# The last image's first residual: its variance by covariance, its sums taken beside other work, and a projection made ahead of the division

## The chip, the cores and the metric

The kernel runs on one core of one Trainium2 chip. The metric is the device time of one execution in microseconds, the median of the runs shown. A core has a matrix engine (PE), a vector engine (DVE), a scalar engine (ACT), a general engine (POOL) and an engine that issues most DMAs (SP). Each executes its instructions in the order of the program, and waits on semaphores of the others.

## The reference

Four images `x` of 256 channels and 64x64 pixels in float32 go through four layers. Each is a residual on a group norm: `x = x + layer(gn(x))`, with 32 groups of 8 channels.

```
gn(v): mean and variance over groups of 8 channels x 4096 pixels
layer 0: xs = relu(group_norm8(conv3x3(v)))
         f = theta(xs)^T phi(xs); y = softmax(f) g(xs)        # 4096 x 4096 per image
         return 0.1 * group_norm8(w_w y) + xs                 # 8 groups of 32 channels
layer 1: linear attention: rmsnorm, q k v, softmax of q over d and of k over n, context, projection, rmsnorm
layer 2: depthwise 3x3 and pointwise 256x256 convolutions with kernels generated from the input
layer 3: a mix of four 256x256 experts, weighted by a softmax from the pooled input
```

The change concerns the end of layer 0 of the last image and the group norm at the head of layer 1: `x1 = x + xs + 0.1 * gn8(w_w y)`, and then mean and variance of `x1` over groups of 8 channels.

## The kernel before

**Tiles.** The 256 channels lie as two halves (`NH` = 2) of 128 partitions, and an image has 4096 columns. A block `q` is 512 queries (eight blocks). A block has 16 steps `m` of 256 keys. In each step PE makes the logits (`logits`, products `pf`, L898), ACT the exponentials `pr` (L899), PE the sum over keys (`py`, L937), and DVE adds the exponentials to `tot` (L124), from which the softmax's sums come.

**The end of a block** is the generator `ended` (L902 to L926), whose pieces are taken in the first steps of the next block. DVE folds `tot` to `inv` (L906); a product with ones, `pss` (L910), gives the sums over partitions; DVE takes the reciprocal (L912) and divides, `yt = py * inv`; PE projects `yt` with the weights `ww_s` to `ps_wy` (L921), ACT copies that to `wt` (L922), DVE takes `bn_stats` of it (L925), and SP writes `wt` to DRAM (`wy_d`).

**The rest of layer 0 and layers 1 to 3** are the generators `nonlocal_out`, `linear_attention`, `generated` and `mixed`, joined in `tail`. `nonlocal_out` norms the projection (`group_finish`, L330 to L356: `bn_aggr`, an averaging product `pm`, `gm` and `ev` on DVE, a second product `pv`, and `rsqrt` on POOL in L217; then `affine`, L365), and adds it to the residual, `big = wy * sc + xs` (in L1009, recorded under the helper's L127), in eight pieces of 128x1024. In the last image `big` is `tpg`, and the residual stays in SBUF in `xp`; the sums of the residual are made by 16 ACT instructions during the last attention (`residual_sums`, L956 to L963), and the variance of the result by eight ACT squares around the mean that is known by then (L1014). `linear_attention` starts with the second `group_finish`; then, for each of eight chunks of 512 columns, ACT norms the tile (`normed`, L1033, squares L1035, DVE adds the halves to `s2`), PE multiplies by the q, k, v weights (L1057) and sums squares over the channels (`norms`, `ps_ss`, L1043, `rinv` on DVE and POOL), ACT makes the exponentials (L1061) and v (L1062), DVE divides q by its sums, and PE turns q and adds to the context (L1076, L1079).

**The order** on every engine is the one in which the program issues its instructions, and is written out by hand. A `Chain` interleaves the tail of image b-1 with the attention of image b, step by step; the last attention runs beside the tail of image 2, and the tail of the last image follows alone (`end`). Sixteen products of image 2's last layer are held back (`held`, `ps_ex` in L1498) and issued in gaps of PE by `fill(n)`; `settle()` issues the additions that belong to them. In the last image's part, 128x1024 tiles are taken in turns from a pool of nine (`k4`) and from four spare pieces of `ra` and `rt`. The last block's `ended` has no further attention to lie beside, and is stepped by the loop:

```
        for part, _ in enumerate(attention):
            if part == 0:
                end.fill(2)
            elif part == 2:
                end.settle()
        run(last)
```

Of the kernel before, what the change touches and what calls it, by code (L numbers as in the profile page):

```python
# [13 lines left out]
P = 128  # L14
# [79 lines left out]
def conv_preact_fast(ctx: ExitStack, tc: tile.TileContext, guard, x, wc, wtpg, ww, wqkv, wout, w1cat, wd2,  # L94
# [235 lines left out]
    def group_finish(st, avg, eps, shift=None):  # L330


        if callable(st):
            mv = st()
        else:
            mv = sp.tile([P, NH, 2], F32, name="mv")
            for h in range(NH):
                nc.vector.bn_aggr(mv[:, h, :], st[:, h, :, :].rearrange("p c s -> p (c s)"))
        if shift is not None:
            tt(mv[:, :, 0], mv[:, :, 0], shift, ALU.add)  # L340
        yield 1
        pm = bank("pm")
        nc.tensor.matmul(pm[:, 0:NH], avg, mv[:, :, 0], start=True, stop=True)
        gm = sp.tile([P, NH], F32, name="gm")
        nc.vector.tensor_copy(gm, pm[:, 0:NH])
        ev = sp.tile([P, NH], F32, name="ev")
        tt(ev, mv[:, :, 0], gm, ALU.subtract)
        tt(ev, ev, ev, ALU.mult)
        tt(ev, ev, mv[:, :, 1], ALU.add)
        yield 1  # L350
        pv = bank("pv")
        nc.tensor.matmul(pv[:, 0:NH], avg, ev, start=True, stop=True)
        rstd = sp.tile([P, NH], F32, name="rstd")
        nc.vector.tensor_scalar(rstd, pv[:, 0:NH], eps, None, ALU.add)  # L354
        rsqrt(rstd, rstd)
        return mv, gm, rstd  # L356
# [530 lines left out]

    def attend(b):

        probs, todo = {}, []  # L890
        st = wy_stats[b] = sp.tile([P, NH, 8, 6], F32, name="wy_st")

        def logits(i):
            q, m = divmod(i, NM)
            pr = k4("pr")
            for s in range(2):
                pf = bank("pf")
                nc.tensor.matmul(pf, phi[:, bass.ts(2 * m + s, P)], theta[:, bass.ts(q, 512)], start=True, stop=True)  # L898
                nc.scalar.activation(pr[:, bass.ts(s, 512)], pf, AF.Exp)  # L899
            probs[i] = pr  # L900

        def ended(q, py, tot):  # L902

            at = b * NQ + q
            inv = wk.tile([P, 512], F32, tag="inv", name="inv")
            nc.vector.scalar_tensor_tensor(inv, tot[:, 0:512], 1.0, tot[:, 512:CH], ALU.mult, ALU.add,  # L906
                                           accum_out=guard[:, 0, at:at + 1])
            yield
            pss = bank("pss")
            nc.tensor.matmul(pss, ones, inv, start=True, stop=True)  # L910
            yield
            nc.vector.reciprocal(inv, pss)  # L912
            yt = k2("yt")
            tt(yt, py, inv, ALU.mult)
            yield
            nc.scalar.activation(junk(), inv, AF.Copy, accum_out=guard[:, 1, at:at + 1])

            wt = k4("wt").rearrange("p (h n) -> p h n", h=NH)
            for h in range(NH):
                ps = bank("ps_wy")  # L920
                nc.tensor.matmul(ps, ww_s[:, bass.ts(h, P)], yt, start=True, stop=True)  # L921
                nc.scalar.copy(wt[:, h, :], ps)  # L922
            yield
            for h in range(NH):
                nc.vector.bn_stats(st[:, h, q, :], wt[:, h, :])  # L925
            nc.sync.dma_start(out=wy_d[b].rearrange("h p n -> p h n")[:, :, bass.ts(q, 512)], in_=wt)  # L926

        logits(0)
        for i in range(NQ * NM):
            q, m = divmod(i, NM)  # L930
            if m == 0:
                py = bank("py")
                tot = k4("tot")
            if i + 1 < NQ * NM:
                logits(i + 1)
            for s in range(2):
                nc.tensor.matmul(py, g[:, bass.ts(2 * m + s, P)], probs[i][:, bass.ts(s, 512)],  # L937
                                 start=(m == 0 and s == 0), stop=(m == NM - 1 and s == 1))
            if m == 1:
                tt(tot, probs[i - 1], probs[i], ALU.add)  # L940
            elif m > 1:
                tt(tot, tot, probs[i], ALU.add)
            for t in todo:
                next(t, None)
            if m == NM - 1:
                todo = [ended(q, py, tot)]
                next(todo[0])
            yield i + 1 < NQ * NM
        for t in todo:
            for _ in t:  # L950
                yield


    res_sum = cp.tile([P, NH], F32, name="res_sum")

    def residual_sums(xs_in):  # L956

        parts = sp.tile([P, NH, N // 512], F32, name="res_parts", bufs=1)
        for h in range(NH):
            for c in range(N // 512):  # L960
                nc.scalar.activation(junk(), xs_in[:, h, bass.ts(c, 512)], AF.Copy, accum_out=parts[:, h, c:c + 1])
                yield
        nc.vector.tensor_reduce(res_sum, parts, AX.X, ALU.add)  # L963


    def nonlocal_out(w, b, big, k4, xs_in):
# [4 lines left out]
        def load_parts(i):  # L971
            c, h = PARTS[i]
            wy = k4("wy")
# [7 lines left out]
        ahead = 2 if xs_in is None else 6  # L981
        parts = [load_parts(i) for i in range(ahead)]
        if xs_in is not None:
            yield 1
        bias = vec_s[:, V_WB, :]
        wmv, gm, rstd = yield from group_finish(wy_stats[b], avg32, 1e-5, bias)
        sc, sh = affine(gm, rstd, vec_s[:, V_G2W, :], vec_s[:, V_G2B, :], bias, 0.1)
        st = stats_tile()
        if xs_in is not None:

            mv = sp.tile([P, NH, 2], F32, name="mv_in", bufs=1)
            centre = sp.tile([P, NH], F32, name="centre", bufs=1)
            squares = sp.tile([P, NH, N // CH], F32, name="squares", bufs=1)
            tt(mv[:, :, 0], wmv[:, :, 0], bias, ALU.subtract)
            tt(mv[:, :, 0], mv[:, :, 0], sc, ALU.mult)
            stt(mv[:, :, 0], res_sum, 1.0 / N, mv[:, :, 0], ALU.mult, ALU.add)
            nc.vector.tensor_scalar(centre, mv[:, :, 0], -1.0, None, ALU.mult)

            def moments():
                nc.vector.tensor_reduce(mv[:, :, 1], squares, AX.X, ALU.add)  # L1000
                nc.vector.tensor_scalar(mv[:, :, 1], mv[:, :, 1], 1.0 / N, None, ALU.mult)
                return mv

            st = moments
        w.fill(2)
        for i, (c, h) in enumerate(PARTS):
            cols = bass.ts(c, CH)
            wy, xs = parts[i]
            stt(big[:, h, cols], wy, sc[:, h:h + 1], xs, ALU.mult, ALU.add)  # L1009
            if i + ahead < len(PARTS):  # L1010
                parts.append(load_parts(i + ahead))
            yield 0.6
            if xs_in is not None:
                nc.scalar.activation(wy, big[:, h, cols], AF.Square, bias=centre[:, h:h + 1], accum_out=squares[:, h, c:c + 1])  # L1014
            else:
                for s in range(2):
                    nc.vector.bn_stats(st[:, h, 2 * c + s, :], big[:, h, bass.ts(2 * c + s, 512)])
            yield 0.6
        w.settle()
        return st, sh  # L1020


    def linear_attention(w, b, big, qT, k4, st, sh, alone):
        _, gm, rstd = yield from group_finish(st, avg8, 1e-5, sh)
# [56 lines left out]

        ahead = normed(0)
        yield 1
        ready = *ahead, None
        last = None
        for c in range(NC):
            if c + 1 < NC:
                ahead = normed(c + 1)
            yield 0.5
# [9 lines left out]
        rk = sp.tile([P, 1], F32, name="rk")  # L1099
# [98 lines left out]
    def generated(w, b, big, k4, st, sh, diag):  # L1198
        mv, gm, rstd = yield from group_finish(st, avg8, 1e-5, sh)

        pivot = sp.tile([P, NH], F32, name="pivot")
# [7 lines left out]
        hs = sp.tile([HT * HP, NC3], F32, name="hs")  # L1209
# [6 lines left out]
        b1n = sp.tile([HT * HP, 1], F32, name="b1n")  # L1216
# [33 lines left out]
        pooled = sp.tile([HT * HP, 1], F32, name="pooled")  # L1250
        nc.vector.tensor_reduce(pooled, hs, AX.X, ALU.add)
        pd = sp.tile([HT * HP, 2 * R], F32, name="pd")
# [5 lines left out]
        pb = sp.tile([P, 2 * R], F32, name="pb")  # L1258
# [3 lines left out]
        dk = sp.tile([P, NH * 9], F32, name="dk")  # L1262
# [177 lines left out]
    def mixed(w, b, big, k4, st, sh, held):  # L1440
# [7 lines left out]
        pool = sp.tile([P, NH], F32, name="rpool")  # L1448
# [6 lines left out]
        hid = sp.tile([EH, 1], F32, name="hid")  # L1455
# [6 lines left out]
        nm = sp.tile([P, 1], F32, name="lnm")  # L1462
        nc.vector.tensor_reduce(nm, pl[:, 0:NE], AX.X, ALU.max, negate=True)
        al = sp.tile([P, NE], F32, name="al")
        asum = sp.tile([P, 1], F32, name="asum")
# [5 lines left out]
        scales = sp.tile([P, NH, NE], F32, name="scales")  # L1471
# [15 lines left out]
        b3 = sp.tile([P, NH], F32, name="b3")  # L1487
# [46 lines left out]
    def tail(b, big, qT, k4=k4, diag=None, xs_in=None, held=None):  # L1534

        def layers(w):
            st, sh = yield from nonlocal_out(w, b, big, k4, xs_in)
            st = yield from linear_attention(w, b, big, qT, k4, st, sh, diag is not None)
# [33 lines left out]
    with tc.manual_schedule(engines={E.PE, E.Activation, E.DVE, E.Pool, E.SP}):  # L1572
# [20 lines left out]
        sums = residual_sums(x_cols)  # L1593
        while next(attention, False):
            for _ in range(3):
                next(sums, None)
        for _ in sums:
            pass
        next(last)
        for part, _ in enumerate(attention):  # L1600
            if part == 0:
                end.fill(2)
            elif part == 2:
                end.settle()
# [586 lines left out]
```

## Time and profile before

| | before |
|---|---|
| median of 3 runs | 3103.75 us (3103.21 to 3104.64) |
| profiled execution, its own time | 3104.24 us |
| its span, first to last instruction | 3102.5 us |
| mean granted PE clock | 0.990 |
| last attention's last `py` product ends | 2820.74 us |
| first q, k, v product of the last image | 2849.59 us |

The page gives the busy time of each engine, the chain of waits that ended last, and groups of instructions. Times in the trace count from the start of the span. An engine's idle time costs something only where that engine, or one waiting for it, is on the chain. The granted clock is the share of PE's full clock that it ran at.

### The profile page before, as it was taken

How to read it: one execution, taken by the hardware profiler on the slowest of the kernel's cores; microseconds unless marked ns; L12 is line 12 of the kernel's file. 1: busy time of each engine (PE TensorE's matmuls, PEld its weight loads, DVE VectorE, ACT ScalarE, POOL GpSimd, SP SyncE). 2: the span in 40 equal slices, each digit the busy share in tenths (PEclk: the TensorE clock that was granted, in tenths of full speed). 3: DMA queues.
4: the chain of work that ended last, by engine and by line, in shares of the span. 5: the costliest groups of instructions: out<-in, count | busy, mean ns of one | idle time of the engine just before them, and what ended most of it. 6: DMA issues, size and time to landing. Idle time of an engine off the chain costs nothing.

```text
span 3102.5 us, 24417 instructions
## 1 busy us (share of the span) xinstructions
PE 3005.3 (97%) x8606; PEld 1486.3 (48%) x8606; DVE 2108.8 (68%) x2713; ACT 1173.3 (38%) x2188; POOL 131.0 (4%) x178
## 2 busy tenths in 40 slices
PE   6899999999999999999999999999999999998998
PEld 3354555445554444444565444444546544444643
DVE  8747777853557986787536897778363668865485
ACT  2134333353555332323364532222445443335621
POOL 0100000000010000000011000000000100000100
PEclk9999999999999999999999999999999999998999
DMA  5233111122100023113300102311420010021021
GB/s 218 79 100 140 34 48 31 34 51 79 51 11 30 12 75 126 38 38 65 115 8 4 34 27 75 115 41 34 95 82 1 11 34 7 16 80 68 8 68 66
DMA packets 58913, 174.25 MB, mean 56 GB/s; under 512 B 6432, under 2 KB 16416, under 8 KB 54560
## 3 DMA queue, kind: packets, MB, share of 16 engines
q1 hardware_dynamic: 54752, 155.85, 14.6%
q0 software_dynamic: 4032, 16.78, 2.9%
q8 instruction: 70, 1.15, 0.2%
q14 instruction: 59, 0.48, 0.1%
HBM read 111.26 MB, written 78.12 MB: 61 GB/s over the span
## 4 chain that ended last, share of the span: by engine, by line
PE 77%; DVE 16%; issue 5%; ACT 1%; DMA 0%; POOL 0%; POOLq 0%; ACTq 0%; DVEq 0%; SPq 0%
PE pf L898 22%; PE py L937 22%; PE ps_qkv L1057 5%; PE ps_conv L499 4%; PE ps_tp L874 4%; DVE dw L127 4%; PE ps_ex L1498 3%; DVE tot L124 3%; PE ps_pw L1298 3%; PE ps_conv L571 2%; PE ps_g L879 2%; PE ps_wy L921 2%; PE ps_o L1125 1%; PE ps_dw L1343 1%; DVE big L127 1%
## 5 line engine op out<-in xcount | busy, mean ns | idle before, releaser
L899 ACT ACTIVATE pr<-pf 128x512 f32<-128x512 f32 x1024 | 603.1, 596 | 1184.5 <-PE pf L898 1138.8
L898 PE MATMUL pf<-tpg 128*128 128x512 f32 x2048 | 969.3, 596 | 2.9 <-ACT pr L899 2.9
L937 PE MATMUL py<-pr,tpg 128*128 128x512 f32 x2048 | 962.3, 592 | 2.5 <-ACT pr L899 2.3
L124 DVE TENSOR_TENSOR tot<-tot,pr 128x1024 f32<-128x1024 f32 x448 | 546.0, 1219 | 181.1 <-ACT pr L899 179.7
L937 PEld LDWEIGHTS py<-pr,tpg 128*128 128x128 f32 x2048 | 388.8, 190 | 494.8 <-issue 476.1
L898 PEld LDWEIGHTS pf<-tpg 128*128 128x128 f32 x2048 | 381.9, 190 | 438.1 <-issue 412.5
L127 DVE SCALAR_TENSOR_TENSOR dw<-xp,dk,dw 128x1008 f32<-128x1008 f32 x208 | 262.9, 1267 | 9.9 <-ACT dw L1290 7.0
L499 PE MATMUL ps_conv<-v,u 128*128 128x512 f32 x384 | 171.0, 593 | 3.6 <-DVE v L124 3.6
L1057 PE MATMUL ps_qkv<-wqkv_s,xg 128*128 128x384 f32 x384 | 129.9, 487 | 0.0
L124 DVE TENSOR_TENSOR tpg<-ps_g,bg_s 128x512 f32<-128x512 f32 x32 | 22.1, 691 | 145.7 <-PE ps_g L879 145.7
L874 PE MATMUL ps_tp<-big,wtpg_s 128*128 128x512 f32 x256 | 118.1, 605 | 3.0 <-ACT big L671 3.0
L499 PEld LDWEIGHTS ps_conv<-v,u 128*128 128x128 f32 x384 | 72.6, 190 | 96.4 <-issue 89.8
L217 POOL TENSOR_TENSOR rstd<-rstd,half 128x2 f32<-128x2 f32 x24 | 16.8, 699 | 2359.6 <-DVE rstd L354 2227.4
L912 DVE RECIPROCAL inv<-pss 128x512 f32<-128x512 f32 x32 | 107.2, 3351 | 7.1 <-PE pss L910 7.1
L1298 PE MATMUL ps_pw<-dw,pk 128*128 128x512 f32 x224 | 101.3, 592 | 0.0
L1057 PEld LDWEIGHTS ps_qkv<-wqkv_s,xg 128*128 128x128 f32 x384 | 72.2, 190 | 53.5 <-issue 9.3
L1067 DVE TENSOR_REDUCE qs<-qk 128x16 f32<-128x512 f32 x24 | 16.5, 686 | 118.6 <-ACT qk L1061 118.6
L875 ACT ACTIVATE tpg<-ps_tp,btp_s 128x512 f32<-128x512 f32 x64 | 43.8, 686 | 119.7 <-PE ps_tp L874 119.7
L874 PEld LDWEIGHTS ps_tp<-big,wtpg_s 128*128 128x128 f32 x256 | 47.9, 195 | 55.0 <-issue 50.6
L1127 ACT ACTIVATE junk<-ps_o 128x256 f32<-128x256 f32 x128 | 49.1, 384 | 63.7 <-PE ps_o L1125 59.4
L1061 ACT ACTIVATE qk<-ps_qkv,rinv 128x256 f32<-128x256 f32 x96 | 45.5, 473 | 72.5 <-PE ps_qkv L1057 61.8
L124 DVE TENSOR_TENSOR v<-ra 128x1024 f32<-128x1024 f32 x58 | 69.5, 1219 | 0.4
(338 smaller groups left out, 3123.8 us busy)
## 6 DMA issues: line engine op xcount, KB each, us to landing
xp<-in_x_dram SPq DMA_DIRECT2D x16, 1024.0 KB, 6.5
wy_d<-wt SPq DMA_DIRECT2D x32, 512.0 KB, 3.0
out_dram<-res SPq DMA_DIRECT2D x64, 256.0 KB, 2.0
wy<-wy_d SPq DMA_DIRECT2D x28, 512.0 KB, 4.7
xs_d<-big POOLq DMA_DIRECT2D x24, 512.0 KB, 11.1
u<-filters SPq DMA_DIRECT2D x48, 256.0 KB, 2.5
xs<-xs_d SPq DMA_DIRECT2D x24, 512.0 KB, 5.4
u<-rows_d SPq DMA_DIRECT2D x36, 256.0 KB, 3.1
```

The costliest lines, as they stand in the source:

```text
L124: nc.vector.tensor_tensor(o, a, b, op)
L127: nc.vector.scalar_tensor_tensor(o, a, s, b, op0, op1)
L499: nc.tensor.matmul(ps[oh], u(oh, h), v[:, bass.ts(h, 512)], start=(h == 0), stop=(h == NH - 1))
L571: nc.tensor.matmul(ps[:, bass.ts(oh, IY * IX)], u[i][:, h, bass.ts(oh, P)], v[:, i, bass.ts(h, IY * IX)], start=(h == 0), stop=(h == NH - 1))
L874: nc.tensor.matmul(ps, wtpg_s[:, h, k, :], big[:, h, cols], start=(h == 0), stop=(h == NH - 1))
L898: nc.tensor.matmul(pf, phi[:, bass.ts(2 * m + s, P)], theta[:, bass.ts(q, 512)], start=True, stop=True)
L899: nc.scalar.activation(pr[:, bass.ts(s, 512)], pf, AF.Exp)
L912: nc.vector.reciprocal(inv, pss)
L937: nc.tensor.matmul(py, g[:, bass.ts(2 * m + s, P)], probs[i][:, bass.ts(s, 512)], start=(m == 0 and s == 0), stop=(m == NM - 1 and s == 1))
L1057: nc.tensor.matmul(ps[:, 0:3 * HID], xg[:, h, bass.ts(j, P)], wqkv_s[:, h, :], start=(h == 0), stop=(h == NH - 1))
L1298: nc.tensor.matmul(ps, pk[:, h * NH * P + oh * P:h * NH * P + (oh + 1) * P], dw[h][:, bass.ts(s, 512)], start=(h == 0), stop=(h == NH - 1))
L1498: nc.tensor.matmul(ps, wm[h][:, bass.ts(oh, P)], big[:, h, bass.ts(c, 512)], start=(h == 0), stop=(h == NH - 1))
```

## The change

In the last attention, each block loads its part of the residual, `xc`, from DRAM into a `k4` slot (step 9), takes `bn_stats` of it (steps 12 and 14), and after the block's projection multiplies it with `wt` minus a pivot (the mean of the first block's projection), with the sum accumulated in `joint`. With these the variance of `wy * sc + xs` is var(wy) sc² + 2 cov sc + var(xs), known before the sum is made. The two multiplies of the last block are issued inside the first `group_finish`. `residual_sums`, the eight squares and the moments from them are gone. The eight additions move into `linear_attention` as the generator `on_the_way`: two pieces of 128x512 inside the second `group_finish`, two after the first `normed`, the others between the chunks. Four tiles are loaded ahead in place of six, all from the pool. In the last block of the last image ACT copies `py` without the division, PE projects that ahead of the reciprocal, and DVE multiplies the product by `inv`. In all images `wt` is allocated earlier, right after `pss`. Some small tiles have one buffer in place of two. The held products are issued at other places.

```diff
-    def group_finish(st, avg, eps, shift=None):
+    def group_finish(st, avg, eps, shift=None, between=()):
...
         tt(ev, ev, mv[:, :, 1], ALU.add)
+        for f in between[0:1]:
+            f()
         yield 1
         pv = bank("pv")
...
         rsqrt(rstd, rstd)
+        for f in between[1:]:
+            f()
         return mv, gm, rstd
...
+        def multiply(q, h, wt, xc):
+            nc.vector.scalar_tensor_tensor(xc[:, h, :], wt[:, h, :], pivot_in[:, h:h + 1], xc[:, h, :], ALU.add, ALU.mult,
+                                           accum_out=joint[:, h, q:q + 1])
+
+        def with_residual(q, wt, xc):
+            if q == 0:
+                mv = sp.tile([P, NH, 2], F32, name="mv")
+                for h in range(NH):
+                    nc.vector.bn_aggr(mv[:, h, :], st[:, h, 0, :])
+                nc.vector.tensor_scalar(pivot_in, mv[:, :, 0], -1.0, None, ALU.mult)
+            if q < NQ - 1:
+                for h in range(NH):
+                    multiply(q, h, wt, xc)
+            else:
+                last_block.extend(lambda h=h: multiply(q, h, wt, xc) for h in range(NH))
...
+            wt = k4("wt").rearrange("p (h n) -> p h n", h=NH)
+            if at == B * NQ - 1:
+                yt = k2("yt")
+                nc.scalar.copy(yt, py)
+                banks = [bank("ps_wy") for _ in range(NH)]
+                for h in range(NH):
+                    nc.tensor.matmul(banks[h], ww_s[:, bass.ts(h, P)], yt, start=True, stop=True)
+                yield
+                nc.vector.reciprocal(inv, pss)
+                for h in range(NH):
+                    tt(wt[:, h, :], banks[h], inv, ALU.mult)
+                nc.scalar.activation(junk(), inv, AF.Copy, accum_out=guard[:, 1, at:at + 1])
+                yield
...
             nc.sync.dma_start(out=wy_d[b].rearrange("h p n -> p h n")[:, :, bass.ts(q, 512)], in_=wt)
+            if b == B - 1:
+                with_residual(q, wt, xc)
...
+            if b == B - 1 and m == 9:
+                xc = k4("xc").rearrange("p (h n) -> p h n", h=NH)
+                nc.sync.dma_start(out=xc, in_=xs_d[b].rearrange("h p n -> p h n")[:, :, bass.ts(q, 512)])
+            if b == B - 1 and m in (12, 14):
+                h = m // 2 - 6
+                nc.vector.bn_stats(res_st[:, h, q, :], xc[:, h, :])
...
-        ahead = 2 if xs_in is None else 6
-        parts = [load_parts(i) for i in range(ahead)]
+        parts = [load_parts(i) for i in range(2 if xs_in is None else 4)]
...
+        if xs_in is not None:
...
+            tt(mv[:, :, 0], wmv[:, :, 0], bias, ALU.subtract)
+            tt(off, mv[:, :, 0], pivot_in, ALU.add)
+            for h in range(NH):
+                nc.vector.bn_aggr(rmv[:, h, :], res_st[:, h, :, :].rearrange("p c s -> p (c s)"))
+            nc.vector.tensor_reduce(cov, joint, AX.X, ALU.add)
+            tt(off, off, rmv[:, :, 0], ALU.mult)
+            stt(cov, cov, 1.0 / N, off, ALU.mult, ALU.subtract)
         sc, sh = affine(gm, rstd, vec_s[:, V_G2W, :], vec_s[:, V_G2B, :], bias, 0.1)
         if xs_in is not None:
...
-            stt(mv[:, :, 0], res_sum, 1.0 / N, mv[:, :, 0], ALU.mult, ALU.add)
-            nc.vector.tensor_scalar(centre, mv[:, :, 0], -1.0, None, ALU.mult)
+            w.fill(1)
             tt(mv[:, :, 0], mv[:, :, 0], sc, ALU.mult)
+            tt(mv[:, :, 0], mv[:, :, 0], rmv[:, :, 0], ALU.add)
+            tt(mv[:, :, 1], wmv[:, :, 1], sc, ALU.mult)
+            stt(mv[:, :, 1], cov, 2.0, mv[:, :, 1], ALU.mult, ALU.add)
+            tt(mv[:, :, 1], mv[:, :, 1], sc, ALU.mult)
+            tt(mv[:, :, 1], mv[:, :, 1], rmv[:, :, 1], ALU.add)
+
+            def on_the_way():
+                for s in range(2):
+                    for h in range(NH):
+                        cols = bass.ts(s, 512)
+                        wy, xs = parts[h]
+                        stt(big[:, h, cols], wy[:, cols], sc[:, h:h + 1], xs[:, cols], ALU.mult, ALU.add)
+                        if s == 0:
+                            yield
+                yield
+                for c in range(1, N // CH):
+                    if c > 1:
+                        parts.extend(load_parts(2 * c + h) for h in range(NH))
+                        yield
+                    for h in range(NH):
+                        added(2 * c + h, sc)
+                    yield
+
+            return (lambda: mv), sh, on_the_way()
...
-            if xs_in is not None:
-                nc.scalar.activation(wy, big[:, h, cols], AF.Square, bias=centre[:, h:h + 1], accum_out=squares[:, h, c:c + 1])
...
-        _, gm, rstd = yield from group_finish(st, avg8, 1e-5, sh)
+        _, gm, rstd = yield from group_finish(st, avg8, 1e-5, sh, (lambda: next(sums),) * 2 if alone else ())
...
+        if alone:
+            w.fill(1)
+        w.settle()
         ahead = normed(0)
+        if alone:
+            next(sums)
...
             if c + 1 < NC:
                 ahead = normed(c + 1)
+            if alone:
+                next(sums, None)
```

## The prediction

> **What bounds the kernel now.** I read the busy table and the slices of the page first, then the chain that ended last, then busy time by windows, and at the end the timelines of PE, DVE and POOL around the end of the last attention.
>
> ```profile
> PE 3005.3 (97%) x8606; PEld 1486.3 (48%) x8606; DVE 2108.8 (68%) x2713; ACT 1173.3 (38%) x2188; POOL 131.0 (4%) x178
> ...
> PE 77%; DVE 16%; issue 5%; ACT 1%; DMA 0%; POOL 0%; POOLq 0%; ACTq 0%; DVEq 0%; SPq 0%
> ```
>
> PE is the bound nearly everywhere, so an edit pays only where PE stands still. The windows say where (columns: window, its length, busy time of each engine, granted clock, DMA share, GB/s).
>
> ```profile
> 2340.00:2540.00 200.00, 200.00 (x696) 108.48 (x695) 102.88 (x154) 103.11 (x227) 21.08 (x20) 1.00 0.04 12
> 2540.00:2600.00 60.00, 60.00 (x141) 26.60 (x140) 54.23 (x52) 22.47 (x38) 0.00 (x0) 1.00 0.09 27
> ...
> 2832.00:2834.00 2.00, 2.00 (x4) 0.97 (x3) 1.27 (x11) 0.00 (x0) 0.52 (x1) 0.50 0.75 186
> ...
> 2850.00:2858.00 8.00, 8.00 (x19) 4.84 (x19) 1.46 (x3) 5.23 (x9) 1.01 (x1) 0.50 0.00 0
> ```
>
> In the last attention (2340 to 2821) PE is busy in 200.00 of 200 and 60.00 of 60 us. DVE has room on average (102.88 of 200) but hardly any between 2540 and 2600 (54.23 of 60). Behind it PE has nothing of its own until the first q, k, v product at 2849.59:
>
> ```profile
> 2821.64 3.37 DVE inv L912
> ...
> 2825.03 0.70 DVE yt L124
> ...
> 2825.77 2.00 PE ps_wy L921 x4
> ...
> 2835.15 8.45 DVE tpg L127 x7
> 2843.60 1.32 DVE res L127 x2
> ...
> 2845.39 0.60 PE pm L343 x2
> ```
>
> The chain (start, length, what) runs over the reciprocal, the division, the last projection, then eight residual adds of 128x1024 from 2833.95, 1.20 us apart, whose squares give the variance that the next norm needs. PE's timeline gives the price in its idle time (brackets), and shows the first q, k, v chunks slow:
>
> ```profile
> 2829.86 0.38 PE L343 MATMUL pm<-mv,avg 128*128 128x2 f32 x2 [2.10 <-DVE mv L124]
> ...
> 2845.39 0.59 PE L343 MATMUL pm<-mv_in,avg 128*128 128x2 f32 x2 [8.69 <-DVE mv_in L124]
> ...
> 2849.59 2.93 PE L1057 MATMUL ps_qkv<-wqkv_s,ra 128*128 128x384 f32 x4 [2.19 <-ACT ra L1033]
> ...
> 2853.88 6.65 PE L1057 MATMUL ps_qkv<-wqkv_s,ra 128*128 128x384 f32 x12
> ...
> 2866.42 0.95 PE L1043 MATMUL ps_ss<-ones,s 128*128 128x1 f32 x8
> ```
>
> From 2866.42 on PE stays busy. So I carry the changed kernel to this third ps_ss, on the clock of before, with the attention ending at 2820.74 as now.
>
> **Projection ahead of the division.** Before: reciprocal to 2825.00, yt, ps_wy, two ACT copies, bn_stats at 2827.55 and 2828.41, bn_aggr at 2829.02. After: ACT copies py (a copy from PSUM is 0.58), and ps_wy is done by about 2824, all beside the reciprocal (3.37). Then DVE alone: two multiplies at 2825.03 and 2825.64 (0.69 long, 0.61 apart as yt and its follower), bn_stats at 2826.25 and 2826.86, bn_aggr at 2827.47. Gain 1.55; pm moves from 2829.86 to 2828.3. The four held products now stand behind ps_wy, and still end before pm.
>
> **Covariance instead of adds.** From pm, gm to ev takes 1.16 and pv follows at 2829.5. Two multiplies with accumulation (the same form as the softmax's fold in L906: 0.69, its accumulator read from 0.62 on for 0.08, so some 0.74 from start to start) are issued around it. The first, at 2829.5, holds rstd until 2830.25 (0.3 lost, as rstd came 0.42 after pv). The second runs from 2830.3 to 2831.0 beside POOL's rsqrt. Then stand seven small operations: 0.20 apart when dependent (the ev rows), 0.07 to 0.12 when not, bn_aggr 0.29 each, in all 1.4. So sc comes at 2832.45 where before it came at 2832.56: the 1.55 is spent. Affine takes 0.73 as before (2832.56 to 2833.29). Then seven operations, mostly dependent, give the mean and variance without the adds: 1.3, and the second pm is at 2834.5, not 2845.39. Gain so far **10.9**. Gone from this stretch are the eight adds (1.20 each), ACT's eight squares (1.15 each) and the two res adds (1.40) between them and the moments; what is late next is the norm's own chain of small operations.
>
> **A rsqrt beside DVE.** From this pm to the first normalized tile took 3.34. Now the first two 128x512 adds stand in that chain; the first fits the wait for pv, the second starts just as POOL's rsqrt does. What that costs, other rsqrt rows show:
>
> ```profile
> 2422.95 1.01 POOL L217 TENSOR_TENSOR zr<-zr,half 128x4 f32<-128x4 f32 x1 [29.96 <-DVE zr L1132]
> ...
> 2440.77 1.91 POOL L217 TENSOR_TENSOR zr<-zr,half 128x4 f32<-128x4 f32 x1 [6.41 <-DVE zr L1132]
> ```
>
> The second ran beside a tot add from 2440.60 to 2441.82 and ended 0.86 after it; the first had DVE idle. If POOL simply waits for the add, the 0.70 rsqrt here ends 0.55 after a 0.69 add begun 0.25 earlier, 0.3 late. Its bounds are 0 and 0.9; I take 0.3. So ACT starts ra at 2838.2 and PE q, k, v at 2839.0, against 2849.59: gain **10.55**. The same lock on the first rsqrt (norm of wy) is covered by the seven small operations. No row here has a two-column rsqrt beside a two-operand add; the Trainium skill, "GPSIMD Engine Reference", Specifications, says that GpSimd's SBUF interfaces are shared with VectorE and contend with instructions of two SBUF inputs, without a size; by it the 0.3 stands, and without it the sum would be 10.85.
>
> **Start of the q, k, v loop.** Chunk 0's s2 is on DVE at 2840.8, behind four res adds (0.65 apart, done 2840.7). Two 128x512 adds follow, so ACT's tile for chunk 1 starts at 2842.1, some 1.3 later than by shift alone; then two 128x1024 adds (2.40) stand ahead of rinv, which comes at 2847.6 instead of 2843.9. ACT's exponentials start at 2848.8, 3.6 late. What does PE do meanwhile? Before, its clock was 0.50 from 2842 to 2858, and chunk 0's last 12 records plus chunk 1's 16 took it from 2853.88 to 2866.42, all busy. The same work shifted runs from 2843.3 to 2855.9; the products fill free banks, and the third bank of chunk 1 waits only for the read of ps_ss at 2847.6. ACT's side (four pairs of 0.75, then 1.54, 1.06, and 0.69 on DVE) has s2 of chunk 2 ready at 2855.0. So PE's half clock covers the DVE delay, with 0.9 to spare, and the third ps_ss comes at 2855.9: gain **10.5**. If the clock were full, PE would be ready by 2853.2 and would wait for ACT: 2855.0, gain 11.4. The later adds (2.40 in chunks 2 and 4) lie in DVE's wait of some 2.75 for ACT in each chunk of 7.33, and loads 4 to 7 land (4.7 in the page) 10 us ahead of their use.
>
> The clock deserves a second look. In the rows it falls to 0.50 in 2832 to 2834 although the longest idle time of PE just before was 2.10, and it stays at 0.50 for 8 us after the q, k, v products began. After the change PE idles in pieces of 1 to 3 us over 2827 to 2839, so I keep the half clock. The Trainium skill, "TensorE: Matmul & The Clock Gate", HAM oscillation, puts the limit at idle gaps above about 3.4 us and the return at about as much of work; by that page the clock would stay full, and the sum would be the 11.4.
>
> **The attention loop** gets per block of 16 steps (55 us): one 512 KB load, two bn_stats (0.69) and two accumulating multiplies (0.74), 2.8 us of DVE, and one of nine slots of the 128x1024 pool held from step 9 to step 3 of the next block; wt is held two steps longer. By rows of 3.43 us a step PE needs ACT's exponentials 1.2 of each, ACT idles half the time. I followed the two tightest places by hand. In block 1, steps 3 and 4 (2325 to 2331), the next probability tile waits for DVE to free xc's slot and comes 2.9 late, but PE has q, k, v work queued until 2333. In block 3 (2537 to 2565) it is 0.6 early. Hence 0, with 0 to 4 as bounds; no gain can hide here as PE is full. Also at nothing: the 16 ACT sums that go (beside a PE at 100%; nothing waits), the smaller pools (their tiles are used once per image, some 700 us apart), the load order on SP.
>
> **Sum.** 3104.24 (profiled; span 3102.5 and 1.74 around it) minus 10.6 is 3093.6; the profiled run is 0.49 above the median, so on the median 3093.2.
>
> **Rivals.** (1) *Slower: a slot held by DVE stalls PE in the attention.* ACT's exponential waits for xc's slot, behind it the next exponentials, and PE's py. For it: the 2.9 late tile above and DVE's 54.23 of 60. Against: it needs PE to be out of queued work. It decides from 0.55 us a block (8 x 0.55 takes the gain under 6.2) and turns the sign from 2.1 a block; at the 2.9 it costs 23.2: 3116. (2) *The start stays cold.* If the DVE delays punch holes into PE's first chunks, the clock returns one chunk later: before, 2849.59 to 2861.18 took 11.6 for a chunk and two ps_ss, at full clock 6.8, so 4.8 more: gain 5.8, 3098. (3) *Shorter than worked out.* Full clock, no lock on POOL, small operations 0.1 apart: 11.4 + 0.3 + 0.9, 3091. (4) *It doesn't do what it says*: the second norm still waits for adds or a load. Order on DVE speaks against it, nothing of the adds stands ahead of pm; 3104.
>
> **Chances.** Forecast 0.60, rival 1 0.12 (0.04 of it within the same), rival 2 0.13 (0.05 faster, 0.08 same), rival 3 0.12, rival 4 0.03. A difference of 0.2% (6.2 us) is about what a measurement of this kernel can tell from none. Faster 0.60 + 0.12 + 0.05 = 0.77; same 0.04 + 0.08 + 0.03 = 0.15; slower 0.08. The range runs from 3088 (rival 3 and 3 us for the unknown spacings) to 3100 (rival 2 and half of the loop's 4), which leaves out rivals 1 and 4 and little more.
>
> **What would show it.** Right: PE idle ahead of the second pm near 3, not 8.69; sc about as late as before; no squares in ACT; POOL's second rstd near 1.0; ACT's first exponential some 9.8 after the first q, k, v product (6.2 before); PE busy all through 2340 to 2821. Wrong: PE idle time released by ACT pr in the last attention, or a third ps_ss that moves by much less than the first q, k, v product.

## The result and the profile after

| | before | after |
|---|---|---|
| median of 8 runs | 3103.78 us (3103.21 to 3104.86) | 3093.36 us (3092.82 to 3095.36) |
| span of the profiled execution | 3102.5 us | 3091.9 us |
| third `ps_ss` of the last image, from the start of the last `pss` | 45.84 us | 33.65 us |
| fourth `ps_ss`, from the same point | 53.18 us | 42.72 us |

The ratio is 0.9967, with a 95% interval of 0.9958 to 0.9976: faster by 10.4 us. From the fourth `ps_ss` to the end both take the same (228.7 us), so the whole gain lies between the last attention and that point, and for the runs below I also count from the start of `pss`, since the attention itself ends up to 1.2 us earlier or later from one execution to the next (`pss` starts between 2820.06 and 2821.76 in the profiles). Behind the fourth `ps_ss`, where most of the edits below change nothing, the profiles of the runs take between 226.5 (run 4) and 229.2 us (runs 5 and 8). So a median alone does not tell an edit's worth to a microsecond.

The busy table and the chain's shares of the changed kernel:

```profile
PE 3001.9 (97%) x8606; PEld 1484.7 (48%) x8606; DVE 2130.8 (69%) x2773; ACT 1152.7 (37%) x2139; POOL 131.9 (4%) x178
...
PE 78%; DVE 15%; issue 5%; ACT 1%; POOL 0%; DMA 0%; POOLq 0%; ACTq 0%; DVEq 0%
```

DVE has 22 us more work and ACT 21 less, and neither is seen in the time. The windows (columns as before; the clock is the third number from the end) show the attention and, behind it, the start of the q, k, v loop between two cold stretches (PE at half clock):

```profile
2340.00:2540.00 200.00, 200.00 (x696) 108.42 (x695) 107.85 (x166) 103.12 (x226) 21.12 (x20) 1.00 0.06 20
2540.00:2600.00 60.00, 60.00 (x141) 26.60 (x140) 56.52 (x58) 22.43 (x38) 0.00 (x0) 1.00 0.11 36
...
2836.00:2838.00 2.00, 2.00 (x3) 0.68 (x2) 1.48 (x5) 0.73 (x2) 1.10 (x2) 0.50 0.00 0
2840.00:2854.00 14.00, 11.23 (x45) 7.03 (x44) 7.45 (x12) 8.15 (x16) 2.07 (x3) 1.00 0.49 153
2856.00:2858.00 2.00, 2.00 (x10) 1.70 (x9) 1.54 (x4) 1.97 (x5) 0.30 (x1) 0.50 0.48 186
```

PE is busy in all of 2340 to 2600, as before. But the q, k, v start, 2840 to 2854, ran at a clock of 1.00, where before it was 0.50, and PE was idle in 2.8 of these 14 us. PE's timeline names the waits:

```profile
2833.80 0.38 PE L344 MATMUL pm<-mv_in,avg 128*128 128x2 f32 x2 [2.10 <-DVE mv_in L124]
2835.02 0.59 PE L355 MATMUL pv<-ev,avg 128*128 128x2 f32 x2 [0.84 <-DVE ev L124]
2835.47 3.38 PE L1574 MATMUL ps_ex<-big,wmh 128*128 128x512 f32 x4
2838.69 1.45 PE L1126 MATMUL ps_qkv<-wqkv_s,ra 128*128 128x384 f32 x4
...
2841.57 4.12 PE L1126 MATMUL ps_qkv<-wqkv_s,ra 128*128 128x384 f32 x12
...
2854.17 1.02 PE L1112 MATMUL ps_ss<-ones,s 128*128 128x1 f32 x8 [2.43 <-DVE s L124]
...
2857.34 6.07 PE L1126 MATMUL ps_qkv<-wqkv_s,rt 128*128 128x384 f32 x16
2863.24 0.95 PE L1112 MATMUL ps_ss<-ones,s 128*128 128x1 f32 x8
```

The wait of 8.69 ahead of the second `pm` is 2.10. The held product behind the second `pv` runs cold (3.38 for four records; 1.96 for the four ahead of it), and the q, k, v products behind it warm (4.12 for 12 records, 6.65 before). Then comes something that the kernel before didn't have: PE waits 2.43 for the third chunk's `s2`, and the 16 records behind that take 6.07 instead of the 5.33 of later chunks. The chain of waits (start, length, what) says where the 2.43 comes from:

```profile
2821.58 3.37 DVE inv L948
2825.04 1.29 DVE wt L124 x2
...
2833.80 0.40 PE pm L344 x2
...
2844.63 2.39 DVE tpg L127 x2
2847.17 1.02 POOL rinv L217
...
2853.33 0.70 DVE s L124
2854.17 1.02 PE ps_ss L1112 x8
```

The two 128x1024 adds, 2.39 us, are on the chain, ahead of `rinv`, and through it ahead of ACT's exponentials and the next tile.

### The profile page after: what moved, and what is told of

Its sections match the earlier page's. It is cut to its first block, busy times and chain, and to the rows that moved or that the text cites. A ratio compares the mean times of both kernels' runs of the same rounds, so it can differ in the third digit from the quotient of the medians.

```text
span 3091.9 us, 24448 instructions
## 1 busy us (share of the span) xinstructions
PE 3001.9 (97%) x8606; PEld 1484.7 (48%) x8606; DVE 2130.8 (69%) x2773; ACT 1152.7 (37%) x2139; POOL 131.9 (4%) x178
## 4 chain that ended last, share of the span: by engine, by line
PE 78%; DVE 15%; issue 5%; ACT 1%; POOL 0%; DMA 0%; POOLq 0%; ACTq 0%; DVEq 0%
PE pf L926 23%; PE py L982 22%; PE ps_qkv L1126 5%; PE ps_conv L504 4%; PE ps_tp L879 4%; DVE dw L127 4%; PE ps_ex L1574 3%; DVE tot L124 3%; PE ps_pw L1374 3%; PE ps_conv L576 2%; PE ps_g L884 2%; PE ps_wy L963 2%; PE ps_o L1201 1%; PE ps_dw L1419 1%; DVE big L127 1%
```

## The experiments

The question is where the 10.4 us come from. Theory A: the adds leave the norm's chain, PE's clock in the q, k, v start follows from PE's idle time just before, and the wait of 2.43 comes from the two adds ahead of `rinv`. The rivals put the gain elsewhere: into the squares and moments that are gone, the clock alone, or the projection. All edits are to the changed kernel, except where it says "the kernel before"; "..." stands for code that is left out. `warm(n)` is n products of 128x384 into a PSUM bank that nobody reads.

**1. The adds ahead of the norm again.**

```diff
-            return (lambda: mv), sh, on_the_way()
+            for i in range(len(PARTS)):
+                added(i, sc)
+                if i + 4 < len(PARTS):
+                    parts.append(load_parts(i + 4))
+            return (lambda: mv), sh, iter(())
...
```

> The changed kernel with its eight residual adds put back in one row behind the covariance's small operations and ahead of the second group norm (eight of 128x1024, 1.20 us apart). Theory A, the gain is that the adds leave the chain: the second pm goes from 2833.8 to about 2843.4, some 2.0 ahead of before's 2845.39, the first q, k, v product to about 2847.6; the start of the q, k, v loop is as slow as before; time 3104 - 2 = 3102. Rival B, the gain is that the squares, the moments and the two res adds ahead of the second norm are gone: then most of the 10.4 us stays, under 3097.

Measured: 3098.35 us (3097.35 to 3099.47), ratio to before 0.9982 [0.9973, 0.9991]. The second `pm` stood where theory A put it, but the time was 3.7 better than it said. PE's timeline:

```profile
2843.13 0.59 PE L344 MATMUL pm<-mv_in,avg 128*128 128x2 f32 x2 [11.66 <-DVE mv_in L124]
...
2845.01 3.52 PE L1576 MATMUL ps_ex<-big,wmh 128*128 128x512 f32 x4
2848.37 1.46 PE L1130 MATMUL ps_qkv<-wqkv_s,ra 128*128 128x384 f32 x4
...
2850.89 4.12 PE L1130 MATMUL ps_qkv<-wqkv_s,ra 128*128 128x384 f32 x12
```

PE idled for 11.66, and still the 12 records took 4.12, not 6.65. What is new is the held product ahead of them. The rival (squares and moments) would have shown in `pm`, and didn't. Counted from `pss`, the fourth `ps_ss` came at 47.94, 5.2 later than with the adds where the change has them.

**2. The same, with the held product ahead of the second `pm`.**

```diff
         if xs_in is not None:
-            w.fill(1)
+            w.fill(2)
...
-        if alone:
-            w.fill(1)
         w.settle()
         ahead = normed(0)
```

> The changed kernel with the eight adds ahead of the second norm and with the held product ahead of the second pm instead of behind the second pv. Theory A, the adds-first kernel came out at 3098.35 instead of 3102 because that product warmed PE: now the q, k, v start runs at half clock, 3101.5 to 3102.5. Rival, the 3.6 us were something else (squares, moments): 3098.4.

Measured: 3101.22 us (3098.89 to 3102.31), 0.9990 [0.9981, 0.9999]. The clock was 0.50 from 2839 to 2854:

```profile
2847.43 2.93 PE L1130 MATMUL ps_qkv<-wqkv_s,ra 128*128 128x384 f32 x4 [2.13 <-ACT ra L1106]
...
2851.72 5.83 PE L1130 MATMUL ps_qkv<-wqkv_s,ra 128*128 128x384 f32 x12
```

Of the 2.9 us between the medians of these two runs, the profiles show 2.4 up to the fourth `ps_ss` (47.94 and 50.34 from `pss`): that is the warm start. What is left against before, 2.5 by the medians and 2.8 by the fourth `ps_ss`, is the earlier projection and the squares and moments together (2.0 by the expectation of run 1).

**3. The kernel before, kept warm.**

```diff
             if xs_in is not None:
+                if i == 3:
+                    warm(12)
                 nc.scalar.activation(wy, big[:, h, cols], AF.Square, ...)
...
+        if alone:
+            warm(2)
         nb = norm_bias(gm, rstd, sh)
...
```

> The kernel before, with 12 products that nobody reads (128x384) on PE during the residual adds and two more behind the second pv, so that PE does not idle for 8.69 us. Theory A, the half clock in the q, k, v start comes from that idle time and matters only in part: the clock is 1.00 from 2842 on, the 12 + 16 records of the first two chunks take about 4.1 + 5.4 us instead of 6.65 + 5.41 at mixed clock, the third ps_ss comes 2 to 3 us earlier (bound then by ACT), time 3101 to 3102. Rival B, the clock is what the change mainly brought: 3094 to 3096. Rival C, the clock does not matter there: 3103.8.

Measured: 3101.60 us (3099.93 to 3102.02), 0.9992 [0.9983, 1.0002], with the 12 records at 4.12. In the profile the fourth `ps_ss` came 49.45 after `pss`, 3.7 ahead of before. The interval takes in no change, so the reading rests on this one profile. Theory A's size, and far from rival B's.

**4. The projection behind the division again.**

```diff
-            if at == B * NQ - 1:
+            if False:
```

> The changed kernel with the last block's projection behind the reciprocal and the division again, as in every other block. Theory A: bn_aggr is 1.55 us later (2829.0 instead of 2827.44), everything behind it shifts by that, time 3093.4 + 1.6 = 3095.0. Rival: the reciprocal hid it already, or the shift is taken up by the PE wait of 2.43 us in the start of the q, k, v loop: 3093.4.

Measured: 3097.13 us (3093.37 to 3097.75), 0.9976 [0.9967, 0.9985], more than twice the cost that was expected. PE's timeline behind the wait:

```profile
2856.82 1.74 PE L1112 MATMUL ps_ss<-ones,s 128*128 128x1 f32 x8 [2.43 <-DVE s L124]
...
2861.02 6.68 PE L1126 MATMUL ps_qkv<-wqkv_s,rt 128*128 128x384 f32 x16
```

From `pss`, the third `ps_ss` came 1.4 later than after, which is the projection; the fourth 3.1 later, because the cold stretch behind the wait lasted from 2856.9 to 2863.8 and not 3.4 us. The 11 runs fall into two groups, two at 3093.4 and nine at 3095.9 to 3097.75. The profile is of the slower group; that the two quick ones had a shorter stretch is only argued.

**5. PE kept busy in the wait of 2.43.**

```diff
             if c + 1 < NC:
+                if alone and c == 1:
+                    warm(3)
                 ready = *ahead, norms(ahead[1])
...
```

> The changed kernel with three products that nobody reads (128x384, some 2.0 us) on PE in the wait of 2.43 us for chunk 2's s2. Theory A, this wait puts PE on half clock for the next 3.4 us (2855.2 to 2858.6 in the profile of the changed kernel) and so costs 1.7 us beyond itself: the third ps_ss stays at 2854.2, the fourth comes at 2861.6 instead of 2863.24, time 3091.7. Rival: the slower records behind the wait come from elsewhere (ACT's copies, banks): 3093.4 or later by what the products take.

Measured: 3091.38 us (3090.93 to 3092.42), 0.9960 [0.9946, 0.9973]. PE's timeline:

```profile
2853.94 1.02 PE L1117 MATMUL ps_ss<-ones,s 128*128 128x1 f32 x8 [0.23 <-DVE s L124]
...
2856.20 5.33 PE L1131 MATMUL ps_qkv<-wqkv_s,rt 128*128 128x384 f32 x16
```

From `pss`, the third `ps_ss` is where it was to 0.2, the 16 records are back at 5.33, and the fourth `ps_ss` comes 1.4 earlier (2.0 in the median), by doing more. So the wait did cost twice: itself, and the cold records behind it.

**6. The held product early, with the adds where the change has them** (the edit of 2 alone).

> The changed kernel with the held product that stands behind the second pv (four records, 2835.5 to 2838.7 in its profile) issued ahead of the second pm instead. Theory A, this product is what warms PE for the q, k, v products, and the changed kernel was as fast as forecast because two errors cancel: without it the start runs at half clock as before, PE covers DVE's delay, there is no wait of 2.43 and no half clock behind it; first q, k, v product some 0.6 earlier, the fourth ps_ss between 2862 and 2864 (2863.24 now), time 3092.5 to 3094.5. Rival, a cold start costs the 3.7 us that it costs the kernel before: 3097.

Measured: 3091.10 us (3090.99 to 3092.61), 0.9958 [0.9945, 0.9972]. This is the path of the forecast:

```profile
2838.64 2.92 PE L1126 MATMUL ps_qkv<-wqkv_s,ra 128*128 128x384 f32 x4 [2.60 <-ACT ra L1102]
...
2842.93 6.19 PE L1126 MATMUL ps_qkv<-wqkv_s,ra 128*128 128x384 f32 x12
...
2855.01 0.95 PE L1112 MATMUL ps_ss<-ones,s 128*128 128x1 f32 x8
2855.82 0.63 PE L1145 MATMUL ps_qt<-ident,rt 128*128 128x128 f32 x4
```

A cold start, PE without a wait at the third `ps_ss`, and no cold stretch behind it. The warm start of the changed kernel bought nothing: PE only came to the wait for DVE earlier. The median is even 2.3 lower, more than the 0.5 by which the fourth `ps_ss` came earlier in this profile (its slowest run); what the other 1.8 are was not shown.

**7. The two 128x1024 adds behind `rinv`.**

```diff
-            if alone:
+            if alone and c > 0:
                 next(sums, None)
...
                 if rinv is None:
                     rinv = norms(s2)
+                    if alone:
+                        next(sums)
```

> The changed kernel with the two 128x1024 adds of columns 1024 to 2047 issued behind rinv of chunk 0 instead of ahead of it. Theory A, rinv behind the adds is what makes PE wait 2.43 us for chunk 2's s2, and the wait then costs half clock for 3.4 us: rinv at about 2844.6 instead of 2846.94, ACT's first exponential at 2845.9 instead of 2848.2, s2 of chunk 2 by 2851, no PE wait at the third ps_ss (2851.6) and no half clock behind it; 2.4 + 1.7 less, time 3089.3. Rival: ACT's tile for chunk 2 then waits for the adds themselves, and the wait only changes its name: 3092 to 3093.4.

Measured: 3090.88 us (3089.48 to 3091.77), 0.9958 [0.9944, 0.9971]. Only 2.5 of the 4.1 came in the median (3.0 by the fourth `ps_ss`). PE's timeline:

```profile
2839.45 2.74 PE L1126 MATMUL ps_qkv<-wqkv_s,ra 128*128 128x384 f32 x4
...
2853.21 1.02 PE L1112 MATMUL ps_ss<-ones,s 128*128 128x1 f32 x8 [0.19 <-DVE s L124]
```

The wait at the third `ps_ss` is down to 0.19. But here the half clock at the start lasted from 2835.2 to 2842, not to 2838.3, and took in the first q, k, v products (2.74 instead of 1.45); the 12 records behind them began 0.86 later from `pss` than after the change. That is most of what is missing in the profile. A second thing shows on POOL, first after the change and then in this run: the rsqrt of 1.01 takes 1.98 when the adds start right behind `rinv`. Here it can have cost PE no more than the 0.19.

```profile
2847.17 1.01 POOL L217 TENSOR_TENSOR rinv<-rinv,half 128x4 f32<-128x4 f32 x1 [10.07 <-DVE rinv L1114]
```

```profile
2845.23 1.98 POOL L217 TENSOR_TENSOR rinv<-rinv,half 128x4 f32<-128x4 f32 x1 [7.70 <-DVE rinv L1114]
```

**8. No add beside the second rsqrt.**

```diff
         tt(mv[:, :, 0], mv[:, :, 0], shift, ALU.add)
+        for f in early:
+            f()
         yield 1
         pm = bank("pm")
...
```

The first 128x512 add is passed as `early`, the second comes between `ev` and `pv`.

> The changed kernel with the first 128x512 add issued while PE makes the second pm and the second one while PE makes pv, so that none stands beside POOL's rsqrt. Theory A, POOL waits for a two-operand DVE instruction: rstd on POOL takes 0.70 instead of 1.09, gm comes up to 0.15 later, nb 0.25 to 0.3 earlier; 3093.1, not to be told from 3093.4 by time. Rival, POOL is slower there for another reason: its 1.09 stays.

Measured: 3094.83 us (3094.06 to 3096.23), 0.9971 [0.9961, 0.9982]. Here the two traces, POOL's timeline after the change and then of this run:

```profile
2830.35 1.04 POOL L217 TENSOR_TENSOR rstd<-rstd,half 128x2 f32<-128x2 f32 x1 [62.23 <-DVE rstd L357]
2835.95 1.09 POOL L217 TENSOR_TENSOR rstd<-rstd,half 128x2 f32<-128x2 f32 x1 [4.56 <-DVE rstd L357]
```

```profile
2837.07 0.70 POOL L217 TENSOR_TENSOR rstd<-rstd,half 128x2 f32<-128x2 f32 x1 [4.66 <-DVE nb L124]
```

From `pm` to the second `nb` it is 2.98 instead of 3.28, the 0.3 expected. By time nothing came of it: the median is 1.5 higher, while the fourth `ps_ss` is 0.2 earlier from `pss`. In the profiled execution `pss` itself was 1.0 later, ahead of anything that was edited, and the part behind the fourth `ps_ss` took 0.5 longer.

**9. Both, 7 and 8.**

> The changed kernel with both: the two 128x1024 adds behind rinv, and no add beside POOL's rsqrt. Theory A: 2.4 + 1.7 + 0.3 less, 3089.0. Rival, as for each of the two alone: 3093.4.

Measured: 3089.07 us (3088.77 to 3091.68), 0.9955 [0.9941, 0.9968]: theory A's number, but not by its steps. The wait is not gone:

```profile
2853.25 1.02 PE L1114 MATMUL ps_ss<-ones,s 128*128 128x1 f32 x8 [0.74 <-DVE s L124]
```

The fourth `ps_ss` came 39.87 after `pss`, 2.85 ahead of the changed kernel and not 4.4, and no earlier than in run 7 (39.68). Another 1.3 of this profile's gain lies behind the fourth `ps_ss` (227.3 against 228.7 us), where nothing was edited.

**10. The `rinv` of chunk 0 ahead of the `s2` of chunk 1, and 8.**

```diff
         for c in range(NC):
+            if alone and c == 0:
+                ps, rinv = first_product(ready[0], ready[1])
+                ready = ready[0], ready[1], (rinv, ps)
             if c + 1 < NC:
                 ahead = normed(c + 1)
...
```

`first_product` issues chunk 0's first q, k, v product and then `norms(s2)`.

> The changed kernel with no add beside the second rsqrt, and rinv of chunk 0 issued ahead of s2 of chunk 1 (DVE waits there for ACT), so that neither the rinv on DVE nor its rsqrt on POOL meets the two 128x1024 adds. Theory A: rsqrt of rinv takes 1.01 (1.98 behind the adds), ACT's first exponential comes right behind the squares of chunk 1, at about 2844, PE has no wait at the third ps_ss: 3088.5. Rival, ACT's tile for chunk 2 waits for the adds: the wait at the third ps_ss stays 0.5 to 1: 3089.1 as with both edits before.

Measured: 3089.48 us (3089.11 to 3090.87), 0.9953 [0.9940, 0.9967]. POOL's rsqrt took 1.01 at 2842.50, and the third `ps_ss` at 2852.09 had no wait. The fourth came 38.92 after `pss`, 3.8 ahead of the changed kernel and the earliest of all runs. In this profile the clock was at 0.50 from 2830.5 to about 2840.7, a stretch three times as long as in the changed kernel; the 12 records began 0.5 later from `pss`, which used up part of the gain.

**11. The same, with PE kept busy ahead of the second `pm`** (three products behind the held one).

> The one before, and three products that nobody reads (128x384, some 2.0 us) on PE ahead of the second pm, where PE idles for 2.10. Theory A: the clock stays full from 2831 to the q, k, v products, the held product behind the second pv takes 1.96 instead of 3.4 to 3.8, the first q, k, v product comes 0.6 to 1.3 earlier; 3087.5. Rival: ACT's normalized tile, not PE, sets that start: 3088.5 as without them.

Measured: 3090.93 us (3089.11 to 3091.77), 0.9956 [0.9942, 0.9970]. The held product took 1.96 and the first q, k, v product came at 2838.16, but then PE waited 0.42 and 0.99 for ACT and DVE, and the 12 records took 5.81: the cold stretch had moved to between 2842 and 2846. Nothing was won: the fourth `ps_ss` came 39.78 after `pss`.

**12. The added DVE work of the attention doubled.**

```diff
-                nc.vector.bn_stats(res_st[:, h, q, :], xc[:, h, :])
+                for _ in range(2):
+                    nc.vector.bn_stats(res_st[:, h, q, :], xc[:, h, :])
...
                 for h in range(NH):
+                    nc.vector.bn_stats(spare_st[:, h, :], xc[:, h, :])
+                for h in range(NH):
                     multiply(q, h, wt, xc)
```

> The changed kernel with DVE's added work of the last attention doubled: two more bn_stats (0.69 each) at steps 12 and 14 and two more ahead of the two multiplies, so that a block has 5.5 us of it instead of 2.8 and the residual's slot is held 1.4 us longer. Theory A, PE has enough work ahead and DVE enough idle time: PE stays busy throughout 2340 to 2821, time 3093.4. Rival, the slot held by DVE stalls PE: up to 1.4 us a block in 7 blocks, 3095 to 3103.

Measured: 3094.20 us (3093.30 to 3096.29), 0.9969 [0.9957, 0.9981]. The windows:

```profile
2340.00:2540.00 200.00, 200.00 (x697) 108.57 (x696) 112.32 (x173) 103.11 (x226) 21.18 (x20) 1.00 0.06 20
2540.00:2600.00 60.00, 60.00 (x142) 26.52 (x141) 59.16 (x63) 22.96 (x38) 0.00 (x0) 1.00 0.11 36
```

DVE is busy in 59.16 of 60, and PE has not lost a tenth, nor from 2600 to 2820. The 0.8 in the median lies within what `pss` moves by between executions (0.7 later here, with the fourth `ps_ss` 42.75 after it, against 42.72).

## Why the prediction was right, and where it wasn't

The time was forecast as 3093.2 and is 3093.36. The mechanism held: the adds left the norm's chain. That the number fits to 0.2 is luck, for not all of its steps were right, and two errors of nearly the same size, 1.75 and 1.74, cancel (below, "The start of the loop"). The sum also takes off 10.6 where its own last step had come to 10.5.

**Projection ahead of the division**: `pm` forecast at 2828.3, measured at 2828.27. Undone (run 4) it costs 1.4 at the third `ps_ss`, near the 1.55.

**Covariance instead of adds**: the mechanism held. `sc` came at 2831.94 (2832.45), the second `pm` at 2833.80 (2834.5); small operations were over-sized by 0.7 in all. The run with the adds put back (1) has that `pm` 9.6 later from `pss`, eight adds of 1.20. The gain at the end is smaller, since the moved adds cost time again in the loop. By the fourth `ps_ss` from `pss`, the way from the kernel before to the changed one splits into 2.8 for the projection, squares and moments (53.18 to 50.34, run 2), 2.4 for the warm start (to 47.94, run 1) and 5.2 for the moved adds (to 42.72). With a cold start on both sides (runs 2 and 6) the moved adds are worth 8.1. One reading of the lines was short: the chain of before also goes over the store and the load of `wt` by DMA (2828.41 to 2835.12), which the forecast's account leaves out. Nothing hung on it, as DVE had no idle time at 2835.15.

**The rsqrt beside DVE**: sized 0.3, and 0.3 by run 8. The 0.70 grew to 1.09; the Trainium skill, "GPSIMD Engine Reference", Specifications, names the contention without a size, and these rows give one for two columns and, with run 7, for four.

**The first q, k, v product**: forecast at 2839.0, measured at 2838.69, but set by another engine: not ACT's tile (its first half ended at 2838.1) but the cold held product in front of it on PE. I had no term for that.

**The start of the loop**: here a step failed. I kept the half clock of before; the trace shows 1.00. What I missed is in the change itself: it moves a held product from ahead of the adds to behind the second `pv`, directly ahead of the q, k, v products, and this one takes the cold time on itself. Run 1 shows it warming the start after 11.66 of idle time, run 2 the start cold without it. It is not chance from one execution to the next: in the nine profiles with the held product in this place and no `warm` ahead of it, the 12 records took 4.12 each time; in the three that have it elsewhere and nothing to keep PE warm (before, runs 2 and 6) they took 6.65, 5.83 and 6.19. The forecast's own figure for a full clock was a third `ps_ss` at 2855.0, bound by ACT and DVE; measured, 2854.17, a gain of 12.25. Then 1.74 went again behind it, where the forecast had nothing: the wait that it had seen coming in that case (1.8, measured 2.43) put PE on half clock once more (run 5 takes the wait away, and the fourth `ps_ss` comes 1.4 earlier). So the term that failed is the clock: half in the sum where it ran full, and nothing in it for the cold records behind the wait. 12.25 less 1.74 is 10.5: a third `ps_ss` 1.75 better than forecast, and 1.74 lost behind it. Run 6, the forecast's path, has neither: its third `ps_ss` came 34.90 after `pss`, a gain of 10.9 where 10.5 was forecast for a cold start.

**The clock rule** that I weighed against the row did not settle it either. The Trainium skill, "TensorE: Matmul & The Clock Gate", HAM oscillation, speaks of idle gaps above some 3.4 us. Here idle times of 2.10 and 0.84 close together were enough, and one of 2.43 alone. What agrees with that figure is the length of the stretches at 0.50: 3.4 us (2835.0 to 2838.3 after), 6.8 (run 4), 10.2 (run 10) and 17.0 (2842.0 to 2859.0 before), multiples of about 3.4.

**The attention loop**: zero, as forecast, and with room (run 12). Rival 1 falls: at twice the load DVE is full from 2540 to 2600 and PE has not waited. The reason given, PE's queued work, was not tested by itself.

**Rival 2** (holes in PE's first chunks costing 4.8 more) came in a small form: one hole, and 1.74 behind it. **Rival 3** was right on the clock and mostly on the small operations (0.7 of its 0.9), and wrong on the lock. **Rival 4** is excluded by the wait ahead of `pm`.

**A better version.** Runs 9 and 10 (3089.07 and 3089.48) beat both kernels: the changed one by some 4 us, 14 to 15 below before. Run 9 only moves four of the adds on DVE; run 10 moves two of them, and chunk 0's first product and `rinv` ahead of the two 128x1024 adds. By the fourth `ps_ss` run 10 is the better one by 0.95; the medians don't tell them apart.

## What to carry to other kernels

Work that leaves a chain has to be followed to where it lands: these adds left the norm's chain (9.6 us) and came back ahead of `rinv`, in a start where DVE and not PE set the pace, for a wait of 2.43 and a cold stretch behind it, so that 5.2 was left of the 9.6. In a stage where PE has gaps, its clock belongs into the sum as a term of its own: ask which product runs in front of the dense ones, and what each remaining gap does to the records behind it. And when the total fits, compare the parts all the same, by an instruction that both traces have (here the third and fourth `ps_ss`, from `pss`).

## What the runs showed of the hardware

- The half clock came in stretches of 3.4 us or multiples of it (3.4, 6.8, 10.2, 17.0). Short idle times of PE could start one: 2.43 in one piece, 2.10 and 0.84 (changed kernel), 1.50 and 0.84 (run 10), and in run 11 even 0.42 and 0.99, while 0.71 and 0.91 in the same place in run 4 did not. Where it began differed between executions of almost the same program: behind the waits of 1.50 and 0.84 the clock fell at 2830.5 in run 10, and in the changed kernel it stayed full until 2834.9, behind two more waits.
- A four-record product at half clock (3.52 instead of 1.96) ahead of dense work was enough to have the 12 q, k, v records of the first chunk at full speed (4.12), after 11.66 of idle time (run 1).
- POOL's rsqrt ended 0.55 (two columns) or 0.86 (four columns) after a DVE instruction with two SBUF operands that had started around it: 1.09 instead of 0.70 and 1.98 instead of 1.01.
